# A written engine order through the first two feed-forward tiles of a two-layer cross-attention kernel

## The chip, the cores and the metric

The kernel runs on one core of a Trainium2 chip. The metric is the device time of one execution in microseconds (us); the time before is the median of three runs. One further execution was recorded by the hardware profiler, and the views quoted here come from it.

The core has a matrix engine (TensorE, "PE" in the profile, with its weight loads as "PEld"), a vector engine (VectorE, "DVE"), an activation engine (ScalarE, "ACT"), a third elementwise engine (GpSimd, "POOL") and a queue that issues transfers (SyncE, "SP").

## The reference

Two layers work on x, 8 batches of 112 tokens of 512 numbers, with a context of 375 rows for each batch. Each step normalises x first and adds its result to x.

```python
x = x + _L0_xattn_ref(_layernorm(x), ctx_2048, mask_BxS2_bk0)
x = x + _L0_ffn_ref(_layernorm(x), L0_ffn_w1, L0_ffn_w2, L0_ffn_w3)
x = x + _L1_xattn_ref(_layernorm(x), ctx_2048, mask_BxS2_ik0, L1_xattn_Wq, ...)
x = x + _L1_ffn_ref(_layernorm(x), L1_ffn_wq_gate, ...)
```

The change concerns the first two lines. Layer 0's attention has one head and no projections; masked scores are left out:

```python
scores = jnp.einsum('bsd,bmd->bsm', hidden_states, memory_tokens) * scale
attn = jax.nn.softmax(scores, axis=-1)
readout = jnp.einsum('bsm,bmd->bsd', attn, memory_tokens)
```

Layer 0's feed-forward rounds its activations to 8-bit steps for each token and its weights to -1, 0 and 1 times their mean magnitude (the straight-through terms change nothing in the value):

```python
def _act_quant(x):
    scale = 127.0 / jnp.clip(jnp.max(jnp.abs(x), axis=-1, keepdims=True), EPS)
    return jnp.clip(jnp.round(x * scale), -128, 127) / scale
def _weight_quant(w):
    scale = 1.0 / jnp.clip(jnp.mean(jnp.abs(w)), EPS)
    return jnp.clip(jnp.round(w * scale), -1, 1) / scale
def _bitlinear(x, w):
    xn = _rmsnorm(x)
    ...
    return jnp.einsum('bsd,hd->bsh', xq, wq)
gate = jax.nn.silu(_bitlinear(x, w1))
up = _bitlinear(x, w2)
return _bitlinear(gate * up, w3)
```

The hidden width is 1408. Layer 1's attention has 16 heads and needs, from the context, the keys and values of all 8 batches.

## The kernel before

The 896 tokens are handled by batch (8 of 112 rows) in layer 0's attention, and in 7 tiles of 128 rows from then on. `xs[i]` is tile i of the SBUF array `tokens`.

**Who decides the order.** Everything is written as a Python program for the engines. For PE and SP the written order is kept throughout. For DVE, ACT and POOL a planner orders the instructions by its own estimates, except inside a region opened with `tc.manual_schedule` that names these engines: there the written order is kept among the region's instructions, though planned ones from outside may be set between them. Before the change, such a region covers batches 1 to 7 of layer 0's attention and ends ahead of the feed-forward.

**Layer 0's attention.** For batch b, `write0` (DVE, L141) writes the normalised tokens h; `transpose0` turns them on PE (L358), with a copy on ACT (L360); `scores0` multiplies with the context (PE, L365 and L367), takes the row maximum (DVE, L371 and L372) and the exponential (ACT, L375); `shares0` inverts the sums (DVE, L380 and L381); `turn0` transposes the exponentials (PE, L387; ACT, L389); `readout0` multiplies with the context once more (PE, L394), adds to x (DVE, L396), and sends the result with a DMA from POOL's queue into `tokens` (L402). The tokens of x lie in three tiles of the pool `work0`: batch 0, batches 1 to 3, batches 4 to 7 (`load_x`).

**Filling PE.** The keys and values of layer 1 don't depend on layer 0. `fill(n)` takes the next n of their 56 steps: a key step is eight matmuls (L176) emptied by ACT (L178), a value step eight larger ones (L183), emptied in this stretch by DVE (L185). They are set between the steps of layer 0 to keep PE at work.

**The weights of layer 0.** `ternary(m)` is a generator for weight matrix m of three, stepped by `steps_of(m, n)`: four steps of Abs with a row sum (ACT, L230), one of totals (a small matmul L234 on PE, then DVE L236 to L240), four of scaling (DVE, L244) and Sign (ACT, L245). The list `BETWEEN` says for each batch b and each of three places n (after the scores, ahead of the fill, after `turn0`) which steps go there: a digit is a weight matrix, "p" a step of `preparing`.

**Preparing a feed-forward tile.** `prepare(i0, i1)` has four steps: batch statistics of the tiles' tokens and the inverse root (DVE, L128 to L119); the normalised tokens (DVE, L141), their squares (ACT, L263) and their largest magnitudes (DVE, L264); the rounding factors, a chain of small DVE operations (L267 to L278); the rounding itself (ACT, L305; DVE, L307). Before, `prepare(0, 2)` is stepped from `BETWEEN`, while `prepare(2, 4)` and `prepare(4, NT)` are written in the loop over tiles and are the planner's to place.

**The feed-forward tile.** `turn_gate0(i)` transposes the rounded tokens (PE, L317; ACT, L319). `gate_up0(i)` takes the hidden width in three blocks; each has a gate group and an up group of four matmuls (L501, two PSUM banks), Silu on ACT (L505) and the product on DVE (L506). It then finds the ranges (ACT L263, DVE L264 and a small chain), and rounds (ACT L512, POOL L515). `turn_down0(i)` transposes the result, and `down0(i)` multiplies with the third matrix (PE, L526) and adds to x (DVE, L528). The pool `ps_mm` has four PSUM banks, which gate, up, keys, values, read-outs and `down0` all share. The pool `work1` of these tiles takes the space that `work0` leaves.

Of the kernel before, what the change touches and what calls it, by code (L numbers as in the profile page):

```python
# [23 lines left out]
F32 = mybir.dt.float32  # L24
# [5 lines left out]
AF = mybir.ActivationFunctionType  # L30
# [32 lines left out]
def two_layers(ctx: ExitStack, tc: tile.TileContext, x, ctxT, ctxN, mask0, mask1, w1, w2, w3,  # L63
# [127 lines left out]
    def fill(n=1):  # L191
        for _ in range(n):
            next(kv_steps, None)
# [17 lines left out]
    with tc.tile_pool(name="w0", bufs=1, side="right") as w0p, \  # L211
# [68 lines left out]
            yield fwd, back  # L280

        rooms = {}

        def prepare(i0, i1):

            write = normaliser(xs[i0:i1], f"ln1{i0}")
            yield
            g = i0 // 4
            if g not in rooms:
                rooms[g] = slab("h1")  # L290
            js = range(i0 - 4 * g, i1 - 4 * g)
            hs = [rooms[g][:, j * D:(j + 1) * D] for j in js]
            qs = rooms[g][:, 4 * D:].bitcast(BF16)
            qs = [qs[:, j * D:(j + 1) * D] for j in js]
            for j in range(i1 - i0):
                write(hs[j], j)
            ranges = quantizers(hs, D, f"q1{i0}", qs)
            next(ranges)
            yield
            fwd, back = next(ranges)  # L300
            b1, b2 = back(means[0], 1), back(means[1], 2)
            yield
            for j in range(i1 - i0):
                backs[i0 + j] = b1[:, j:j + 1], b2[:, j:j + 1]
                nc.scalar.activation(hs[j], hs[j], AF.Identity, bias=rounder,  # L305
                                     scale=fwd[:, j:j + 1])
                nc.vector.tensor_scalar_sub(qs[j], hs[j], ROUND)  # L307
                q1[i0 + j] = qs[j]
            yield

        def transposed_h(q, n, name, pool):
            qT = pool.tile([P, n // P, P], BF16, name=f"{name}_qT", bufs=2)
            for c0 in range(0, n // P, 6):
                k = min(6, n // P - c0)
                pt = ps_s.tile([P, 6, P], BF16, name="s")
                for i in range(k):
                    nc.tensor.transpose(pt[:, i, :], q[:, (c0 + i) * P:(c0 + i + 1) * P],  # L317
                                        ident_h)
                nc.scalar.copy(qT[:, c0:c0 + k, :], pt[:, :k, :])  # L319
            return qT  # L320
# [5 lines left out]
        with tc.tile_pool(name="work0", bufs=2, side="right") as work0:  # L326
# [5 lines left out]
            cNs, normal, h0, hT0, s0, eT0 = {}, {}, {}, {}, {}, {}  # L332

            def load_x(b0, b1):
                t = work0.tile([T, b1 - b0, D], F32, name=f"x0_{b0}", bufs=1)
                nc.sync.dma_start(out=t, in_=x[b0:b1].rearrange("b t d -> t b d"))
                x0.extend(t[:, b, :] for b in range(b1 - b0))

# [95 lines left out]
            for i in range(4):  # L434
# [9 lines left out]

            BETWEEN = ["", "", "000", "0", "0", "1", "1", "0", "0", "0", "0", "1", "1", "1", "1",
                       "1", "1", "1p", "p", "2", "2p", "p", "2", "2"]
            preparing = prepare(0, 2)

            def between(b, n):
                for m in BETWEEN[3 * b + n]:
                    if m == "p":
                        next(preparing)
                    else:
                        steps_of(int(m), 1)

            with tc.manual_schedule(engines={ENGINES.PE, ENGINES.SP, ENGINES.DVE,
                                             ENGINES.Activation, ENGINES.Pool}):
                between(0, 2)  # L460
                for b in range(1, B):
                    if b < B - 1:
                        write0(b + 1)
                    scores0(b)
                    between(b, 0)
                    shares0(b)
                    if b > 1:
                        readout0(b - 1)
                    if b + 1 < B:
                        load_ctxN(b + 1)  # L470
                    if b + 2 < B:
                        cTs[b + 2] = load_ctxT(b + 2)
                    elif b + 2 == B:
                        cTs[2] = load_ctxT(2)
                    if b == 2 or b == 4:
                        load_raw(2, b // 2 - 1)
                    if b < B - 1:
                        transpose0(b + 1)
                    between(b, 1)
                    fill(1)  # L480
                    turn0(b)
                    between(b, 2)
                fill(1)
                turn_gate0(0)

                nc.scalar.activation(stat.tile([T, 1], F32, name="top"), s0[B - 1][1], AF.Silu)
                readout0(B - 1)


        with tc.tile_pool(name="work1", bufs=2, side="right") as work1:  # L490
            q3 = {}

            def gate_up0(i):
                qT = q1[i]
                gu = work1.tile([P, H], F32, name="gu")
                for n0, n in HBLK:
                    gate = ps_mm.tile([P, 512], F32, name="mm")
                    up = ps_mm.tile([P, 512], F32, name="mm")
                    for ps, w in ((gate, wqs[0]), (up, wqs[1])):
                        for kc in range(KC):  # L500
                            nc.tensor.matmul(ps[:, :n], lhsT=qT[:, kc, :],  # L501
                                             rhs=w[:, kc * H + n0:kc * H + n0 + n],
                                             start=(kc == 0), stop=(kc == KC - 1))
                    act = work1.tile([P, 512], F32, name="act")
                    nc.scalar.activation(act[:, :n], gate[:, :n], AF.Silu, scale=backs[i][0])  # L505
                    nc.vector.scalar_tensor_tensor(gu[:, n0:n0 + n], up[:, :n], backs[i][1],  # L506
                                                   act[:, :n], ALU.mult, ALU.mult)
                q = work1.tile([P, H], BF16, name="q3")
                ranges = quantizers([gu], H, "q3", [q])
                next(ranges)  # L510
                fwd, back = next(ranges)
                nc.scalar.activation(gu, gu, AF.Identity, bias=rounder, scale=fwd)  # L512
                for n0 in (0, H // 2):
                    cols = slice(n0, n0 + H // 2)
                    nc.gpsimd.tensor_scalar(q[:, cols], gu[:, cols], -ROUND, 1.0,  # L515
                                            ALU.add, ALU.mult)
                q3[i] = q, back

            def turn_down0(i):
                q3[i] = transposed_h(q3[i][0], H, "q3", work1), q3[i][1]  # L520

            def down0(i):
                qT, back = q3[i]
                o = ps_mm.tile([P, D], F32, name="mm")
                for hc in range(HC):
                    nc.tensor.matmul(o, lhsT=qT[:, hc, :], rhs=wqs[2][:, hc * D:(hc + 1) * D],  # L526
                                     start=(hc == 0), stop=(hc == HC - 1))
                nc.vector.scalar_tensor_tensor(xs[i], o, back(means[2], 3), xs[i], ALU.mult, ALU.add)  # L528

            for i in range(NT):  # L530
                if i == 2:
                    list(prepare(4, NT))
                gate_up0(i)
                if i == 0:
                    steps_of(2, 1)
                fill(1)
                if i == 0:
                    turn_gate0(1)
                    list(prepare(2, 4))
                fill(1)  # L540
                if i == 0:
                    steps_of(2, 1)
                elif i == 1:
                    steps_of(2, 2)
                if i:
                    turn_down0(i - 1)
                if 0 < i < NT - 1:
                    turn_gate0(i + 1)
                if i:
                    fill(1)  # L550

                if i == 1:
                    steps_of(2, 1)
                elif i == 2:
                    down0(0)
                if i > 1:
                    down0(i - 1)
                if i == 4:
                    wq_s = slab("wq")[:, :KC * D].rearrange("p (k d) -> p k d", k=KC)
                    nc.sync.dma_start(out=wq_s, in_=wq)  # L560
            write = normaliser(xs[:3], "ln2a")
            for i in range(3):
                transpose2(i, write, i, work1, ps_s)
            turn_down0(NT - 1)
            write = normaliser(xs[3:5], "ln2b")
            transpose2(3, write, 0, work1, ps_s)
            down0(NT - 1)
# [433 lines left out]
```

## Time and profile before

| | us |
|---|---|
| median of 3 runs | 538.13 (537.45 to 540.0) |
| the profiled execution | 537.93 |
| its span, from first to last instruction | 536.1 |
| PE busy | 516.8 |
| DVE busy | 312.1 |
| ACT busy | 247.2 |
| POOL busy | 91.4 |

The span is what the program's instructions cover; about 1.8 us lie around it. In the rows of the profile a name such as L176 is a line of the kernel; "x8" counts instructions; a bracket such as [1.54 <-DVE h L141] is idle time of the engine just ahead of the row and what ended it. A row of several matmuls is one that merges neighbours, so its length is a stretch and not the time of one.

### The profile page before, as it was taken

The numbers are of one execution on the slowest core, as the hardware profiler recorded it, in microseconds if no ns is written. First come the engines' busy times: TensorE is split into PE (matmuls) and PEld (weight loads), VectorE is DVE, ScalarE is ACT, GpSimd is POOL, SyncE is SP. The second block draws the span as 40 slices with busy tenths as digits, with TensorE's granted clock in tenths as the row PEclk, the third lists the DMA queues.
The fourth block names the chain that finished last, engine by engine and source line by source line (L and its number), as shares of the span: only waits on it lengthen the run. The fifth ranks groups of instructions, "written<-read, shape, count | busy, mean of one in ns | idle before, by whom it ended". The sixth has DMA issues, their size and how long they took to land.

```text
span 536.1 us, 8884 instructions
## 1 busy us (share of the span) xinstructions
PE 516.8 (96%) x3430; PEld 315.0 (59%) x3430; DVE 312.1 (58%) x769; ACT 247.2 (46%) x439; POOL 91.4 (17%) x197
## 2 busy tenths in 40 slices
PE   8998998989999999999999999999999999999995
PEld 6544554544455554545565555565654688889984
DVE  2552458769834755544546657988985764434432
ACT  1234754759644444402576545556766233203320
POOL 0000210101111101140121033523653540000000
PEclk9998999999999999999999999999999999999999
DMA  8994976300010120240123202102221000010001
GB/s 246 333 404 172 354 257 244 97 17 0 15 44 1 60 117 1 78 159 0 40 71 90 79 2 70 40 2 70 80 78 42 1 2 0 1 59 21 0 21 44
DMA packets 13312, 45.76 MB, mean 85 GB/s; under 512 B 1985, under 2 KB 2512, under 8 KB 12112
## 3 DMA queue, kind: packets, MB, share of 16 engines
q1 hardware_dynamic: 11744, 41.17, 22.5%
q0 software_dynamic: 1360, 3.96, 2.2%
q8 instruction: 29, 0.48, 0.4%
q14 instruction: 19, 0.16, 0.1%
q10 hardware_dynamic: 160, 0.01, 0.0%
HBM read 41.46 MB, written 1.84 MB: 81 GB/s over the span
## 4 chain that ended last, share of the span: by engine, by line
PE 82%; DVE 9%; issue 2%; ACT 2%; DMA 2%; POOL 2%; ACTq 0%; DVEq 0%; POOLq 0%
PE mm L183 14%; PE s L849 13%; PE mm L176 13%; PE down L867 7%; PE mm L648 5%; PE mm L600 5%; PE mm L501 4%; PE s L734 4%; PE mm L526 3%; PE s L365 3%; PE den L754 3%; PE mm L394 3%; PE num L759 2%; DMA tokens<-x 2%; DVE e L739 1%
## 5 line engine op out<-in xcount | busy, mean ns | idle before, releaser
L176 PE MATMUL mm<-cT,wk 128*128 128x375 f32 x256 | 88.8, 493 | 0.8 <-ACT act L505 0.8
L183 PE MATMUL mm<-wv,cT 128*125 128x512 f32 x192 | 86.8, 598 | 0.0
L740 ACT ACTIVATE e<-e 125x448 f32<-125x448 f32 x96 | 54.0, 574 | 45.3 <-DVE e L739 44.1
L849 PE MATMUL s<-h4T,w 128*128 128x512 f32 (+1 forms) x352 | 72.5, 367 | 1.2 <-DVE ln_f L95 1.2
L739 DVE TENSOR_SCALAR e<-s,upper 125x448 f32<-125x448 f32 x96 | 58.9, 677 | 18.8 <-PE s L734 18.8
L849 PEld LDWEIGHTS s<-h4T,w 128*128 128x128 f32 x352 | 63.5, 188 | 9.7 <-issue 1.8
L176 PEld LDWEIGHTS mm<-cT,wk 128*128 128x128 f32 x256 | 47.2, 192 | 29.2 <-issue 1.3
L183 PEld LDWEIGHTS mm<-wv,cT 128*125 128x125 f32 x192 | 34.8, 187 | 39.1 <-issue 37.5
L867 PE MATMUL down<-w,gu 128*128 128x512 f32 x154 | 37.0, 397 | 0.0
L501 PE MATMUL mm<-w_q,q_qT 128*128 128x512 fp8e4 (+1 forms) x168 | 34.6, 361 | 1.5 <-ACT act L505 1.5
L867 PEld LDWEIGHTS down<-w,gu 128*128 128x128 f32 x154 | 28.7, 188 | 6.6
L723 POOL TENSOR_SCALAR w<-raw 128x512 fp32r<-128x512 int32 (+1 forms) x35 | 22.3, 647 | 58.3 <-ACT w L721 57.9
L857 ACT CAST gu<-gu 128x512 fp32r<-128x512 f32 (+1 forms) x22 | 12.5, 568 | 40.5 <-DVE gu L855 40.5
L721 ACT ACTIVATE w<-raw,zero_point 128x512 fp32r<-128x512 int32 (+1 forms) x35 | 24.2, 694 | 10.6 <-DMA raw<-in_wd_dram 7.2
L734 PE MATMUL s<-qT,kv 32*125 32x112 f32 x768 | 28.5, 279 | 0.2
L501 PEld LDWEIGHTS <-q_qT 128*128 128x128 bf16 x168 | 16.4, 98 | 20.1 <-issue 2.8
L855 DVE SCALAR_TENSOR_TENSOR gu<-s,su,gu 128x512 f32<-128x512 f32 (+1 forms) x22 | 15.1, 684 | 22.2 <-PE s L849 20.2
L515 POOL TENSOR_SCALAR q<-gu 128x704 bf16<-128x704 f32 x14 | 10.9, 798 | 97.7 <-ACT gu L512 97.7
L734 PEld LDWEIGHTS s<-qT,kv 32*125 32x125 f32 x768 | 23.9, 183 | 6.2 <-issue 4.6
L759 PEld LDWEIGHTS num<-e,kv 125*32 125x32 f32 x768 | 20.5, 110 | 11.5 <-issue 11.0
L648 PE MATMUL mm<-wo,qT 128*128 128x512 f32 x56 | 25.8, 603 | 0.9 <-DVE qT L772 0.8
L402 POOL DMA_DIRECT2D tokens<-x x14 | 9.2, 657 | 100.0 <-DVE x L396 62.4
(210 smaller groups left out, 738.8 us busy)
## 6 DMA issues: line engine op xcount, KB each, us to landing
cT<-in_ctxT_dram SPq DMA_DIRECT2D x14, 750.0 KB, 5.6
raw<-in_w_dram SPq DMA_DIRECT2D x6, 1408.0 KB, 18.1
cN<-in_ctxN_dram SPq DMA_DIRECT2D x8, 768.0 KB, 4.7
raw<-in_wd_dram SPq DMA_DIRECT2D x11, 256.0 KB, 2.7
raw<-in_wg_dram SPq DMA_DIRECT2D x10, 256.0 KB, 2.9
raw<-in_wu_dram SPq DMA_DIRECT2D x10, 256.0 KB, 2.9
out_dram<-d SPq DMA_DIRECT2D x7, 256.0 KB, 2.0
wk<-in_wk_dram SPq DMA_DIRECT2D x2, 512.0 KB, 8.2
```

The costliest lines, as they stand in the source:

```text
L176: nc.tensor.matmul(ps, lhsT=wk_s[:, kc, dc * P:(dc + 1) * P], rhs=cT[:, kc, :], start=(kc == 0), stop=(kc == KC - 1))
L183: nc.tensor.matmul(ps, lhsT=cT[:, kc, c * CK:(c + 1) * CK], rhs=wv_s[:, kc, :], start=(kc == 0), stop=(kc == KC - 1))
L501: nc.tensor.matmul(ps[:, :n], lhsT=qT[:, kc, :], rhs=w[:, kc * H + n0:kc * H + n0 + n], start=(kc == 0), stop=(kc == KC - 1))
L600: nc.tensor.matmul(ps, lhsT=wq_s[:, kc, dc * P:(dc + 1) * P], rhs=h2T[g][:, kc, :], start=(kc == 0), stop=(kc == KC - 1))
L648: nc.tensor.matmul(ps, lhsT=qT[:, kc, i * P:(i + 1) * P], rhs=wo_s[:, kc, :], start=(kc == 0), stop=(kc == KC - 1))
L721: nc.scalar.activation(t, raw, AF.Square, bias=zero_point, accum_out=squares[:, k:k + 1])
L734: nc.tensor.matmul(ss[r][:, dc, :], lhsT=kT[rows, dc, c * CK:(c + 1) * CK], rhs=qT[rows, dc, b * T:(b + 1) * T], start=True, stop=True)
L739: nc.vector.tensor_scalar(e, ss[r], upper[:, c, b:b + 1], -CLIP, ALU.min, ALU.max)
L740: nc.scalar.activation(e, e, AF.Exp, scale=SC1)
L759: nc.tensor.matmul(num[r * HD:(r + 1) * HD, dc, :], lhsT=v[:, c, head], rhs=es[r][:, dc, :], start=(c == 0 and dc == 0), stop=(c == NCK - ...
L849: nc.tensor.matmul(ps[:, :n], lhsT=w[:, c:c + P], rhs=h4T[k][:, kc, :n], start=(kc == 0 and k == 0), stop=(kc == KC - 1 and k == 1))
L867: nc.tensor.matmul(ps, lhsT=gus[k][:, hc, j * P:(j + 1) * P], rhs=w[:, c:c + D], start=(hc == 0 and k == 0), stop=(hc == HC - 1 and k == 1))
```

## The change

The written region, which ended ahead of the feed-forward, is kept open in an `ExitStack` named `written` until after tile 1. Inside it, the three preparations are made ahead in a list `preparing`, and "P" in `BETWEEN` steps the second, as "p" steps the first. `gate_up0` is cut in three: `gate_up0` alone, `ranges0` and `round0`. Tiles 0 and 1 are written out, and the loop begins at tile 2. `write0` goes from one batch ahead to two. The tokens of batches 4 to 7 go from the pool `work0` into `w0p`, which lives until the end of layer 0's feed-forward. The order of the matmuls on PE is the same but for the totals of the first two weight matrices.

```diff
@@ prepare / load_x
         rooms = {}
+        written = ExitStack()
...
+        preparing = [prepare(0, 2), prepare(2, 4), prepare(4, NT)]
...
             def load_x(b0, b1):
-                t = work0.tile([T, b1 - b0, D], F32, name=f"x0_{b0}", bufs=1)
+
+                pool = w0p if b1 == B else work0
+                t = pool.tile([T, b1 - b0, D], F32, name=f"x0_{b0}", bufs=1)
@@ the batches
-            BETWEEN = ["", "", "000", "0", "0", "1", "1", "0", "0", "0", "0", "1", "1", "1", "1",
-                       "1", "1", "1p", "p", "2", "2p", "p", "2", "2"]
-            preparing = prepare(0, 2)
+            BETWEEN = ["", "", "000", "0", "1", "01", "1", "0", "0", "0", "0", "1", "1", "1", "1",
+                       "1", "1p", "", "p", "2", "2p", "p", "2P", "2"]
...
-            with tc.manual_schedule(engines={ENGINES.PE, ENGINES.SP, ENGINES.DVE,
-                                             ENGINES.Activation, ENGINES.Pool}):
-                between(0, 2)
-                for b in range(1, B):
-                    if b < B - 1:
-                        write0(b + 1)
-                    scores0(b)
...
+            written.enter_context(tc.manual_schedule(engines={
+                ENGINES.PE, ENGINES.SP, ENGINES.DVE, ENGINES.Activation, ENGINES.Pool}))
+            write0(2)
+            between(0, 2)
+            for b in range(1, B):
+                scores0(b)
+                between(b, 0)
+                shares0(b)
+                if b > 1:
+                    readout0(b - 1)
+                if b + 2 < B:
+                    write0(b + 2)
...
+            fill(1)
+            turn_gate0(0)
+
+            nc.scalar.activation(stat.tile([T, 1], F32, name="top"), s0[B - 1][1], AF.Silu)
+            next(preparing[1])
+            readout0(B - 1)
@@ gate_up0
+                q3[i] = gu
+
+            def ranges0(i):
+                gu = q3[i]
                 q = work1.tile([P, H], BF16, name="q3")
                 ranges = quantizers([gu], H, "q3", [q])
                 next(ranges)
-                fwd, back = next(ranges)
+                q3[i] = gu, q, *next(ranges)
+
+            def round0(i):
+                gu, q, fwd, back = q3[i]
                 nc.scalar.activation(gu, gu, AF.Identity, bias=rounder, scale=fwd)
@@ the tiles
-            for i in range(NT):
+            gate_up0(0)
+            next(preparing[1])
+            ranges0(0)
+            steps_of(2, 1)
+            fill(1)
+            turn_gate0(1)
+            next(preparing[1])
+            steps_of(2, 1)
+            round0(0)
+            fill(1)
+            steps_of(2, 1)
+            gate_up0(1)
+            ranges0(1)
+            steps_of(2, 1)
+            fill(1)
+            round0(1)
+            fill(1)
+            turn_down0(0)
+            turn_gate0(2)
+            steps_of(2, 1)
+            fill(1)
+            next(preparing[2])
+            written.close()
+            for i in range(2, NT):
                 if i == 2:
-                    list(prepare(4, NT))
+                    list(preparing[2])
                 gate_up0(i)
-                if i == 0:
-                    steps_of(2, 1)
-                fill(1)
...
+                ranges0(i)
+                round0(i)
+                fill(2)
+                turn_down0(i - 1)
+                if i < NT - 1:
+                    turn_gate0(i + 1)
                 fill(1)
...
```

More of the change, by code (lines that the diff above doesn't have):

```diff
@@ L443, in two_layers @@
             normal[2] = normaliser(x0[4:], "ln0c")
-            BETWEEN = ["", "", "000", "0", "0", "1", "1", "0", "0", "0", "0", "1", "1", "1", "1",
-                       "1", "1", "1p", "p", "2", "2p", "p", "2", "2"]
-            preparing = prepare(0, 2)
+            BETWEEN = ["", "", "000", "0", "1", "01", "1", "0", "0", "0", "0", "1", "1", "1", "1",
+                       "1", "1p", "", "p", "2", "2p", "p", "2P", "2"]
             def between(b, n):
                 for m in BETWEEN[3 * b + n]:
-                    if m == "p":
-                        next(preparing)
+                    if m in "pP":
+                        next(preparing["pP".index(m)])
@@ L455, in between @@
                     else:
                         steps_of(int(m), 1)
-            with tc.manual_schedule(engines={ENGINES.PE, ENGINES.SP, ENGINES.DVE,
-                                             ENGINES.Activation, ENGINES.Pool}):
-                between(0, 2)
-                for b in range(1, B):
-                    if b < B - 1:
-                        write0(b + 1)
-                    scores0(b)
[L465 to L479, printed above, removed]
-                    fill(1)
-                    turn0(b)
-                    between(b, 2)
-                fill(1)
-                turn_gate0(0)
-                nc.scalar.activation(stat.tile([T, 1], F32, name="top"), s0[B - 1][1], AF.Silu)
-                readout0(B - 1)
@@ new lines, in two_layers @@
+            written.enter_context(tc.manual_schedule(engines={
[10 more added lines that the diff above has]
+                    write0(b + 2)
+                if b + 1 < B:
+                    load_ctxN(b + 1)
+                if b + 2 < B:
+                    cTs[b + 2] = load_ctxT(b + 2)
+                elif b + 2 == B:
+                    cTs[2] = load_ctxT(2)
+                if b == 2 or b == 4:
+                    load_raw(2, b // 2 - 1)
+                if b < B - 1:
+                    transpose0(b + 1)
+                between(b, 1)
+                fill(1)
+                turn0(b)
+                between(b, 2)
@@ L528, in down0 @@
                 nc.vector.scalar_tensor_tensor(xs[i], o, back(means[2], 3), xs[i], ALU.mult, ALU.add)
-            for i in range(NT):
+            gate_up0(0)
[22 more added lines that the diff above has]
+            for i in range(2, NT):
                 if i == 2:
-                    list(prepare(4, NT))
+                    list(preparing[2])
                 gate_up0(i)
-                if i == 0:
-                    steps_of(2, 1)
-                fill(1)
[L537 to L554, printed above, removed]
+                ranges0(i)
[4 more added lines that the diff above has]
+                    turn_gate0(i + 1)
+                fill(1)
+                if i == 2:
                     down0(0)
-                if i > 1:
-                    down0(i - 1)
+                down0(i - 1)
                 if i == 4:
```

## The prediction

> **What bounds the kernel now.** I read the page first. Part 1 puts TensorE at 96% of a span of 536.1 us, and its second line of digits is 8 or 9 in every slice but the last: there is no stretch in which another engine carries the kernel. So an edit is worth what it takes from, or adds to, the time in which TensorE stands; and what TensorE loses once is not made up later.
>
> ```profile
> PE 516.8 (96%) x3430; PEld 315.0 (59%) x3430; DVE 312.1 (58%) x769; ACT 247.2 (46%) x439; POOL 91.4 (17%) x197
> ...
> PEclk9998999999999999999999999999999999999999
> ```
>
> The one 8 in the clock line is the slice from 40 to 54 us. Next, the waits of PE between 0 and 300 us (line waited for, total us, times, longest), without the start-up:
>
> ```profile
> PE s L234 <- ACT w_q L230: 2.3, 1, 2.3
> PE s L358 <- DVE h L141: 1.5, 1, 1.5
> PE mm L501 <- ACT act L505: 1.5, 1, 1.5
> ...
> PE mm L176 <- ACT act L505: 0.8, 1, 0.8
> ```
>
> All four lie in the stretch that the change rewrites. The timeline of PE shows the first, and that it costs more than its 2.35 us: the eight matmuls after it take 4.35 us where the same eight take 2.70 at 61.28.
>
> ```profile
> 38.68 0.60 PE L358 MATMUL s<-ident,h 112*128 112x112 f32 x4
> 41.63 0.39 PE L234 MATMUL s<-w_rows,ones 128*128 128x4 f32 x2 [2.35 <-ACT w_q L230]
> 41.87 4.35 PE L176 MATMUL mm<-cT,wk 128*128 128x375 f32 x8
> 46.02 0.63 PE L387 MATMUL s<-ident,e 112*125 112x112 f32 x3
> ```
>
> ScalarE's timeline has the third wait's cause (L505 waits for the tokens' DMA), and then the order in which it empties PSUM banks: L178 (keys) as soon as they are there, L505 in between, L512 (rounding) later.
>
> ```profile
> 113.59 1.27 ACT L505 ACTIVATE act<-mm,q_back 128x512 f32<-128x512 f32 x2 [3.72 <-DMA tokens<-x]
> ...
> 122.30 0.55 ACT L178 ACTIVATE kv<-mm,bk 128x375 f32<-128x375 f32 x1
> 122.76 0.67 ACT L505 ACTIVATE act<-mm,q_back 128x512 f32<-128x512 f32 x1
> ...
> 124.69 1.55 ACT L512 ACTIVATE gu<-gu,rounder,q_fwd 128x1408 f32<-128x1408 f32 x1
> ```
>
> [...] half speed from about 42.9 to 46.3, after the 2.35 us wait, and none after the waits of 1.5. [...]
>
> **What the change removes.** Each gain is a stretch between two PE starts, less the same stretch elsewhere.
> (A) The totals of the first weight matrix go behind a fill and behind turn0(1). Transposes to the next scores are 38.68 to 46.48 = 7.80; with a totals in it and no wait, 69.72 to 73.24 = 3.52. ScalarE ends the fourth Abs at 41.58, the fill covers that: gain 4.28. One Abs of the second matrix comes a step earlier; that matrix was not waited for at 47.05, and I charge nothing, with ScalarE's idle time before 46 as cover.
> (B) write0 goes an iteration ahead, and prepare(0,2) a step; prepare(2,4), which the planner had put into the same queue, goes to the last batch. The transpose then finds its h, written some 8 us before. 85.89 to 90.70 = 4.81 against 76.16 to 79.21 = 3.05: gain 1.76. The extra write0 per iteration (0.54 on DVE, ahead of nothing PE needs within 5 us) costs nothing. The DMA issues on SP (contexts, weights) and on POOL (tokens) keep their order and their places between the batches.
> (C) The tokens of batches 4 to 7 lie outside the space that act reuses. 109.18 to 115.62 = 6.44 against tile 3's 156.14 to 160.89 = 4.75: gain 1.69. The preparation in the last batches (two squares of 0.62, two maxima of 0.68, 13 small operations) lies beside read-out and fill, and ends about 1 us after gate_up0(0) begins, before its third block needs a bank.
> Sum 7.73: gate_up0(0) starts at about 103.14 and ends at 107.89.
>
> **What it adds.** Count from E, the end of tile 0's last product on DVE (L506), 0.89 after gate_up0 ends, as at tile 3. The written order now puts into DVE, one after another:
>
> ```profile
> 161.81 1.62 DVE L264 TENSOR_REDUCE q_mx<-gu 128x1 f32<-128x1408 f32 x1
> 163.37 0.15 DVE L267 TENSOR_SCALAR q_ss<-q_ss 128x1 f32<-128x1 f32 x1
> ...
> 165.87 0.16 DVE L274 SCALAR_TENSOR_TENSOR q_fwd<-q_fwd,q_y 128x1 f32<-128x1 f32 x1
> ```
>
> These rows are tile 3's, where nothing is interleaved: L506's end to the start of L512 takes 4.34. In tile 0, nineteen dependent small operations of prepare(2,4) stand ahead. Thirteen such start within 2.18 us at 28.45, so 0.18 each: 3.45. The factor of tile 0 is ready at E+7.8. Behind it: three operations of the totals 0.55, two L307 0.85, L244 0.94: E+10.15. ScalarE does Sign (L245, 1.40) only then, ahead of round0(0) (L512, 1.5): E+13.1. **Only behind that** stands the evacuation of the second key fill (L178, 0.55): E+13.65.
> PE comes sooner: totals, fill, transposes and fill took 115.62 to 121.18 = 5.56, and three groups of gate_up0(1) take 2.60, so it wants the fourth group's bank at E-0.89+8.16 = E+7.27. All four banks are then held: by the fill, and by three groups whose activations also queue behind it. Stall 6.4. Then another Sign (1.40) and L505 (0.67) free the fifth group at E+15.75, L506 (0.75) the sixth at E+16.5, and gate_up0(1) ends at E+17.15. Without a stall it would be E+9.42: 7.73 are lost here, by chance the sum gained. Before lost 0.94 here (121.18 to 126.87 against 4.75), so a lead of 0.94 is left.
> In tile 1 the chain is again in ScalarE's order. E1 = E+18.04; +4.34 factor, +0.94 L244, +1.40 Sign, +0.55 key, +1.5 round, +1.35 and +0.58 copies: the last, which gate_up0(2) reads, ends at E+28.75. PE needs 10.38 (126.87 to 137.25) and comes at E+27.53. Stall 1.2, so gate_up0(2) starts at 108.78+28.75 = 137.53 against 137.25: 0.28 late.
> Unknown costs, bounded. The clock: a 6.4 us stall takes it to half; the fifth and sixth groups (0.65 each) pay between 0 and 1.3. I take 0.65. Tile 2: prepare(4,7)'s first step (three L128, aggregates and the small chain, 4.35) is written ahead of gate_up0(2)'s first product. It starts at E+28.4 and ends at E+32.75; the sixth group then waits 0.75. If the planner puts three writes (0.5 each) and three maxima (0.6 each) ahead too, it waits 4.05. I take 2.4. A gain is excluded for both, since neither takes work away.
> Sum: 0.28 + 0.65 + 2.4 = 3.3 us longer, between 1.0 and 5.7. The profiled execution was 537.93 (span 536.1 and 1.8 around it), the median 538.13; the 0.2 between them is below everything here, so 538.13 + 3.3 = 541.5, with its own range 539.1 to 543.9.
>
> **Rivals.** *The gain stays* (529.5 to 535). If ScalarE reaches that key evacuation by E+7.3 instead of E+13.1, nothing stalls: 538.13-7.73-0.94 = 529.5. It decides at 6 us of queue time; half of it gives some 534. For it: every gain is a plain wait in the trace, while the loss is my walk through queues that do not exist yet, with operations in a row where the trace mostly shows them interleaved (0.07 apart). Against: L244 and both reductions are long rows, and three of four banks would still wait for L505.
> *One more wait* (543 to 546). Another of work0's tiles lies under act, so (C) stays, and DVE is backed up further in tile 2, where preparation of three tiles (about 8 us), tile 2's ranges (4.3) and two L528 (1.5) fall into some 14 us of PE.
> *The change doesn't do what it says* (537 to 540): if planned work still slips into the written stretch, as batch statistics did at 84 us, (B) and the stall both shrink.
>
> **Numbers.** About 0.5% (2.7 us) is what a measurement can tell from no change. Forecast 0.60: a third of it ends under 540.8 (same 0.19, slower 0.41). Gain stays 0.29, all faster. One more wait 0.07, slower. Does not do what it says 0.04, same. So faster 0.29, same 0.23, slower 0.48. The range, 531.5 to 545, leaves out the best part of the second case and the worst of the third.
>
> **What will show it.** (A): no 8 in the clock line at 40 us, L234 without a wait. (B): no wait of L358 for h. (C): no wait of L505 for tokens. The stall: PE waits 5 to 7 us in gate_up0(1) for L178 or L505, with L512 ahead of L178 on ScalarE, and an 8 or less in the clock slice at 120 us. Tile 2: waits of L501 for L319 and L506. I am wrong if L178 of the second fill comes before L512, or if PE waits under 2 us there.

## The result: no difference, though tile 0 ends eight microseconds earlier

| | before | after |
|---|---|---|
| median, us | 537.98 (20 runs) | 538.04 (20 runs, 537.08 to 538.71) |
| span of the profiled execution | 536.1 | 535.8 |
| ratio after / before | | 1.0003, 95% interval 0.9995 to 1.001 |

The forecast was 541.5. The executions of the kernel before are mostly of two kinds by granted clock: of the 39 that stood beside the first experiments below, 18 at 0.997 or 0.998 have a median of 537.2 us, and 18 at 0.994 or 0.995 one of 538.3.

The kernel after has line numbers of its own. In a feed-forward tile the matmuls L507, Silu L511, the product L512 and the rounding L525 are L501, L505, L506 and L512 of before; L306, L308, L320 and L322 are L305, L307, L317 and L319; the scores L370 are L365. The single parts below that start from the kernel before keep its numbers or are one off.

On the page of the kernel after, the line of the engines and that of the granted clock are these (columns: busy us, share of the span, instructions; then tenths in 40 slices of 13.4 us):

```profile
PE 516.7 (96%) x3430; PEld 314.3 (59%) x3430; DVE 316.0 (59%) x769; ACT 247.1 (46%) x439; POOL 93.4 (17%) x197
...
PEclk9999999997999999999999999999999999999999
```

The 8 at 40 us has gone, and a 7 has come at 121 us, a place where before had none. The waits of PE up to 300 us after (line waited for, us, times, longest) say the same:

```profile
PE mm L507 <- ACT kv L178: 5.5, 1, 5.5
```

The four waits of 2.3, 1.5, 1.5 and 0.8 us shown of before are all gone; one of 5.5 us is new. PE's timeline after (start, us, what ran), first at the old place of the totals, then at tiles 0, 1 and 2:

```profile
38.81 2.71 PE L176 MATMUL mm<-cT,wk 128*128 128x375 f32 x8
...
41.67 0.30 PE L234 MATMUL s<-w_rows,ones 128*128 128x4 f32 x2
...
102.78 4.92 PE L507 MATMUL mm<-w_q,q_qT 128*128 128x512 fp8e4 x24
107.53 0.28 PE L234 MATMUL s<-w_rows,ones 128*128 128x4 f32 x2
...
121.31 4.64 PE L507 MATMUL mm<-w_q,q_qT 128*128 128x512 fp8e4 x12 [5.47 <-ACT kv L178]
125.75 3.36 PE L176 MATMUL mm<-cT,wk 128*128 128x375 f32 x8
...
137.04 4.93 PE L507 MATMUL mm<-w_q,q_qT 128*128 128x512 fp8e4 x24 [0.17 <-ACT q_qT L322]
141.81 1.45 PE L183 MATMUL mm<-wv,cT 128*125 128x512 f32 x3
```

The same places before:

```profile
115.62 0.28 PE L234 MATMUL s<-w_rows,ones 128*128 128x4 f32 x2
...
126.87 2.79 PE L176 MATMUL mm<-cT,wk 128*128 128x375 f32 x8 [0.77 <-ACT act L505]
...
137.25 4.92 PE L501 MATMUL mm<-w_q,q_qT 128*128 128x512 fp8e4 x24
```

Take the start of the next row as the end of a group. `gate_up0(0)` ends at 107.53, where before it ended at 115.62: 8.09 us of lead. Tile 1 ends at 125.75 (126.87 before: 1.12 left), tile 2 starts at 137.04 (137.25: 0.21 left) and ends at 141.81 (142.01: 0.20 left). From there on both kernels do the same, and the spans differ by 0.3. So eight microseconds were won ahead of tile 0 and given back within tiles 0 and 1. ScalarE's timeline after shows where:

```profile
117.88 1.47 ACT L245 ACTIVATE w_q<-raw,unrounder 128x1408 fp8e4<-128x1408 f32 x1 [4.87 <-DVE raw L244]
119.25 1.54 ACT L525 ACTIVATE gu<-gu,rounder,q_fwd 128x1408 f32<-128x1408 f32 x1
120.70 0.56 ACT L178 ACTIVATE kv<-mm,bk 128x375 f32<-128x375 f32 x1
```

ScalarE stands for 4.87 us with a Sign at the head of its queue that waits for VectorE. The key fill, finished on PE at 113.09, has its bank emptied (L178) only behind that Sign and behind the rounding (L525). PE's next group needs this bank. ScalarE is idle in these 4.87 us, while the finished bank waits from 113.09 to 120.70; it is held by the row at the head of its written order. That row's input is late on VectorE, whose timeline has the scaling that Sign reads only behind the chains of small operations for tiles 2 and 3 and for tile 0, whose factor is the first row here:

```profile
115.70 0.16 DVE L274 SCALAR_TENSOR_TENSOR q_fwd<-q_fwd,q_y 128x1 f32<-128x1 f32 x1
...
116.90 1.81 DVE L244 TENSOR_SCALAR raw<-raw,w_scale 128x1408 f32<-128x1408 f32 x2
```

### The profile page after: what moved, and what is told of

Its sections match the earlier page's. It is cut to its first block, busy times and chain, and to the rows that moved or that the text cites. A ratio compares the mean times of both kernels' runs of the same rounds, so it can differ in the third digit from the quotient of the medians.

```text
span 535.8 us, 8871 instructions
## 1 busy us (share of the span) xinstructions
PE 516.7 (96%) x3430; PEld 314.3 (59%) x3430; DVE 316.0 (59%) x769; ACT 247.1 (46%) x439; POOL 93.4 (17%) x197
## 4 chain that ended last, share of the span: by engine, by line
PE 86%; DVE 8%; ACT 3%; POOL 1%; issue 1%; DVEq 0%; POOLq 0%
PE mm L183 14%; PE s L871 13%; PE mm L176 12%; PE down L889 7%; PE mm L507 6%; PE mm L670 5%; PE mm L622 5%; PE mm L399 4%; PE s L370 4%; PE s L756 4%; PE mm L539 3%; PE den L776 3%; PE num L781 2%; DVE e L761 1%; PE s L428 1%
## 5 line engine op out<-in xcount | busy, mean ns | idle before, releaser
L176 PE MATMUL mm<-cT,wk 128*128 128x375 f32 x256 | 87.7, 488 | 0.0
L176 PEld LDWEIGHTS mm<-cT,wk 128*128 128x128 f32 x256 | 47.1, 191 | 28.1 <-issue 1.2
L507 PE MATMUL mm<-w_q,q_qT 128*128 128x512 fp8e4 (+1 forms) x168 | 36.8, 376 | 5.7 <-ACT kv L178 5.5
L507 PEld LDWEIGHTS <-q_qT 128*128 128x128 bf16 x168 | 16.8, 101 | 26.0 <-issue 9.0
L407 POOL DMA_DIRECT2D tokens<-x x14 | 11.8, 843 | 90.9 <-DVE x L401 62.9
```

The source lines that it names most:

```text
L176: nc.tensor.matmul(ps, lhsT=wk_s[:, kc, dc * P:(dc + 1) * P], rhs=cT[:, kc, :], start=(kc == 0), stop=(kc == KC - 1))
L507: nc.tensor.matmul(ps[:, :n], lhsT=qT[:, kc, :], rhs=w[:, kc * H + n0:kc * H + n0 + n], start=(kc == 0), stop=(kc == KC - 1))
```

## The experiments

Two theories stood against each other. **Order**: the gains ahead of tile 0 are real and add up, and the written order of tiles 0 and 1 gives them back. **Work**: VectorE and ScalarE have too much to do beside PE in these tiles, so any earlier start ends in a wait there, whatever the order. Each run below stood beside runs of the kernel before on the same chip (538.05 or 538.13); ratios are to those.

### The gains one at a time

**a_totals**: the kernel before, with the totals of the first weight matrix behind the fill and `turn0(1)`; the nine steps of the second matrix each come one place earlier, and the preparation stays where it was.

```diff
-BETWEEN = ["", "", "000", "0", "0", "1", "1", ... "1", "1", "1p", "p", ...
+BETWEEN = ["", "", "000", "0", "1", "01", "1", ... "1", "1", "p", "p", ...
```

> The kernel before with only the totals of the first weight matrix moved behind the fill and turn0 of batch 1 (one Abs of the second matrix a step earlier, one step of prepare a place later); the rest stays the planner's. Theory (each wait taken away is worth its own length, and the change gave the sum back in tiles 0 and 1): PE no longer waits 2.35 us for L230 and the clock stays full, so 4.3 us shorter, about 533.7. Rival (something later sets the time, so an earlier gain is lost anyway): within 1 us of 538.

Measured 534.67, ratio 0.9947 (0.9926 to 0.9968). PE's timeline:

```profile
38.75 0.60 PE L358 MATMUL s<-ident,h 112*128 112x112 f32 x4
39.19 2.71 PE L176 MATMUL mm<-cT,wk 128*128 128x375 f32 x8
...
42.05 0.30 PE L234 MATMUL s<-w_rows,ones 128*128 128x4 f32 x2
42.20 2.76 PE L365 MATMUL s<-cT,hT 128*112 128x375 f32 x8
```

No bracket, and the eight L176 take 2.71 (4.35 before, with a granted clock of 0.50 from 44 to 46 us). Transposes to the next scores: 3.45 us instead of 7.80. Of these 4.35 us, 3.4 reach the median. The next run shows one reason for the rest: the half clock behind the 2.35 us wait, worth 1.6 of them, is missing in that trace.

**c_tokens_pool**: the kernel before, with only the tokens of batches 4 to 7 in `w0p`.

```diff
-t = work0.tile([T, b1 - b0, D], F32, name=f"x0_{b0}", bufs=1)
+pool = w0p if b1 == B else work0
+t = pool.tile([T, b1 - b0, D], F32, name=f"x0_{b0}", bufs=1)
```

> The kernel before with only the tokens of batches 4 to 7 in the pool w0p. Theory: the wait of L505 for the tokens' DMA goes and with it 1.7 us of PE in gate_up0(0), about 536.3; the planner's order behind it may take some of that. Rival: another tile of work0 lies under act, the wait stays, 538.

Measured 536.43, ratio 0.9969 (0.9957 to 0.9981). The gain is 1.6. PE's timeline, at the totals and at tile 0 (L502 is L501 of before):

```profile
42.26 0.38 PE L234 MATMUL s<-w_rows,ones 128*128 128x4 f32 x2 [2.35 <-ACT w_q L230]
42.50 2.77 PE L176 MATMUL mm<-cT,wk 128*128 128x375 f32 x8
...
108.39 4.92 PE L502 MATMUL mm<-w_q,q_qT 128*128 128x512 fp8e4 x24
113.15 0.28 PE L234 MATMUL s<-w_rows,ones 128*128 128x4 f32 x2
```

PE no longer waits for the first activation of tile 0: 108.39 to 113.15 is 4.76, against 6.44 before. The first two rows are not the edit's doing: the wait for the totals is as long as before (2.35), but the eight matmuls behind it take 2.77 and not 4.35, at a granted clock of 1.00. So this gain is read from the medians and from tile 0, not from the two spans.

**b_write_ahead**: the kernel before, with only `write0` two batches ahead and one "p" a place earlier.

```diff
-BETWEEN = [... "1", "1", "1p", "p", ...
+BETWEEN = [... "1", "1p", "1", "p", ...
+write0(2)
 between(0, 2)
 for b in range(1, B):
-    if b < B - 1:
-        write0(b + 1)
     scores0(b)
...
         readout0(b - 1)
+    if b + 2 < B:
+        write0(b + 2)
```

> Only (B): write0 two batches ahead and the second step of the first preparation one place earlier; the totals, the tokens' pool and the tiles as before. Theory (the three gains are separate waits and add up): the wait of L358 for h goes, 1.76 us by my sum, 536.4; what the two other single parts leave of close_early's 6.1 us (6.1 - 3.4 - 1.6) says 1.1, 537.0. Rival (the h is late for another reason, the preparation that the planner still sets into VectorE's queue): the wait of 1.5 us stays, 538.1.

Measured 539.44, ratio 1.0023 (1.0012 to 1.0034): **slower**, and neither theory had it. PE's timeline has the wait for h gone, and two others in its place:

```profile
93.48 0.58 PE L387 MATMUL s<-ident,e 112*125 112x112 f32 x3 [0.96 <-ACT e L375]
95.12 2.78 PE L365 MATMUL s<-cT,hT 128*112 128x375 f32 x8 [1.06 <-ACT hT L360]
```

VectorE's timeline of the same run says why (before, these two rows start at 86.78 and 90.12):

```profile
86.88 0.69 DVE L128 BATCH_NORM_STATS2 bn<-tokens 128x6 f32<-128x512 f32 x1 [3.73 <-DMA tokens<-x]
...
91.23 0.54 DVE L371 TENSOR_REDUCE top<-s 112x1 f32<-112x375 f32 x1
```

`prepare(2, 4)` is the planner's in this kernel, and it was set into the queue so early that VectorE stands 3.73 us for the tokens' transfer (0.28 at this row before). A value copy (L185) and a scaling (L244), which before ran ahead of the statistics, now come behind their chain of small operations and ahead of the row maximum L371 of scores that were finished at 86. So (B) is worth its 1.76 only together with the set place for that preparation; the change has both, and the stretch that was 4.81 before takes 3.05 in the kernel after (81.25 to 84.30).

### Keeping the gains, with the tiles left to the planner

**close_early**: the kernel after, with the written region closed behind `readout0(B - 1)`; tiles 0 and 1 have the same PE order as after, and the planner orders the other engines.

```diff
         next(preparing[1])
         readout0(B - 1)
+        written.close()
...
             next(preparing[2])
-            written.close()
```

> The changed kernel with the written region ended ahead of gate_up0(0), so that the planner orders tiles 0 and 1 as it did before; the earlier totals, the earlier write0, the earlier preparation and the tokens' pool stay. The planner's order of ScalarE has one Sign ahead of the second key evacuation, where the written one had two roundings, Sign and round0(0), but it has the squares and roundings of tiles 4 to 6 ahead of the activations of gate_up0(2). Theory: the lead of 8 us shrinks by 1 to 3 us in tile 1 and 3 to 5 in tile 2, 532 to 536. Rival (a planned order has no cost here): 529.5.

Measured 532.01, ratio 0.9883 (0.9868 to 0.9898): the lower end of what was expected. PE's waits inside the tiles are small:

```profile
PE mm L507 <- ACT act L511: 1.4, 2, 0.8
...
PE mm L507 <- DVE kv L185: 0.5, 1, 0.5
```

The planner's order of ScalarE has the second key fill emptied at 115.53, where the written one had it at 120.70:

```profile
115.53 0.56 ACT L178 ACTIVATE kv<-mm,bk 128x375 f32<-128x375 f32 x1
```

The same instructions on the same engines, but for the order of DVE, ACT and POOL in two tiles: 6.0 us between this and the kernel after. This is against **Work**.

### Which place in the order

**key_first**: after, with the second key fill directly behind `turn_gate0(1)`, so that L178 stands ahead of Sign and rounding.

```diff
 turn_gate0(1)
+fill(1)
 next(preparing[1])
 steps_of(2, 1)
 round0(0)
-fill(1)
```

> The changed kernel with the second key fill of tile 0 written ahead of the rounding of tiles 2 and 3, of Sign and of round0(0): PE's order is the same, ScalarE empties that bank at once. Theory (all of ScalarE's queue is late, not one bank): the stall of 5.5 us only moves from the fourth group of gate_up0(1), where it ended with L178, to the fifth, where it ends with L511; one group of 0.87 us gets done ahead of it, so 0.4 to 0.9 us shorter, 537.1 to 537.6. Rival (that one evacuation is the bound): most of 5.5 us comes back, 532.5 to 534.

Measured 538.04, ratio 1.0001 (0.999 to 1.0012). In the waits of PE the stall is as long, one bank later:

```profile
PE mm L507 <- ACT act L511: 6.1, 1, 6.1
```

L511 of tile 1 is now what stands behind Sign, rounding and Sign. That the stall would move was expected; the half microsecond of gain was not found.

**gate_first**: after, with the fill and all of `gate_up0(1)` ahead of both Signs and `round0(0)`.

```diff
 turn_gate0(1)
+fill(1)
 next(preparing[1])
+gate_up0(1)
 steps_of(2, 1)
 round0(0)
-fill(1)
 steps_of(2, 1)
-gate_up0(1)
```

> The changed kernel with the second key fill and gate_up0(1) written ahead of both Sign steps and of round0(0), nothing else moved; PE's order is the same. Theory (ScalarE's order, not PE's, sets these tiles): gate_up0(1) stalls less than 1 us, and ends some 7 us earlier, but the rounding and Sign steps put off now end before tile 2's copy all the same, so PE stalls 5 to 6 us ahead of gate_up0(2), and 1 to 2 us of the whole are left: 536 to 537. Rival (the stall in gate_up0(1) was the whole loss): 530 to 532.

Measured 537.6, ratio 0.9992 (0.9985 to 0.9999). PE's timeline:

```profile
134.50 4.91 PE L507 MATMUL mm<-w_q,q_qT 128*128 128x512 fp8e4 x16 [5.67 <-DVE ln_b L107]
```

Tile 1 runs without a wait, and the stall has gone to the next tile, as expected; of the 1 to 2 us that were to be left of the whole, the medians have 0.4. The releaser that the bracket names is not the one: what `gate_up0(2)` reads is the last copy of ScalarE, and ScalarE's timeline has it behind a Sign that waited for VectorE:

```profile
129.30 1.47 ACT L245 ACTIVATE w_q<-raw,unrounder 128x1408 fp8e4<-128x1408 f32 x1 [3.64 <-DVE raw L244]
...
132.58 1.86 ACT L322 COPY q_qT<-s 128x768 bf16<-128x768 bf16 x3
```

The copies end at 134.44, and PE starts at 134.50. It is the chain that the forecast gave for tile 1, here with nothing ahead of it to hide it.

**hold_tile2**: after, with `gate_up0(2)` inside the written region, behind the first step of `prepare(4, NT)`. This puts to the test the forecast's last term, in which that step stands ahead of tile 2's products.

```diff
+            gate_up0(2)
             written.close()
             for i in range(2, NT):
                 if i == 2:
                     list(preparing[2])
-                gate_up0(i)
+                else:
+                    gate_up0(i)
```

> The changed kernel with the written region ended behind gate_up0(2) instead of ahead of it: the three products of that tile can no longer slip between the batch statistics of tiles 4 to 6. Theory (that slip is why the 2.4 us forecast for tile 2 did not come): a wait of 0.8 to 2 us in gate_up0(2), 538.8 to 540. Rival (the statistics have room there in any order): 538.0.

Measured 539.09, ratio 1.0016 (1.0008 to 1.0025). The waits of PE:

```profile
PE mm L183 <- DVE gu L512: 1.2, 1, 1.2
```

VectorE's timeline has the three products only behind the whole step:

```profile
142.79 2.08 DVE L512 SCALAR_TENSOR_TENSOR gu<-mm,q_back,act 128x512 f32<-128x512 f32 x3
```

This is the wait that the forecast had put into the kernel after, one group later (at the value fill behind the tile); it comes on top of the 5.5 us for L178, and the median is 1.05 us above that of the kernel after.

### An order that keeps the gains

**reordered**: the ranges of tile 0 ahead of the preparation, both key fills ahead of the rounding, totals and scalings of the third matrix behind `gate_up0(1)`; what follows tile 1's steps is planned.

```diff
             gate_up0(0)
-            next(preparing[1])
             ranges0(0)
             steps_of(2, 1)
             fill(1)
             turn_gate0(1)
+            fill(1)
             next(preparing[1])
-            steps_of(2, 1)
             round0(0)
-            fill(1)
-            steps_of(2, 1)
             gate_up0(1)
-            ranges0(1)
-            steps_of(2, 1)
+            next(preparing[1])
             fill(1)
-            round0(1)
+            steps_of(2, 2)
+            ranges0(1)
             fill(1)
             turn_down0(0)
             turn_gate0(2)
+            round0(1)
             steps_of(2, 1)
             fill(1)
-            next(preparing[2])
             written.close()
             ...
                 gate_up0(i)
+                if i == 2:
+                    steps_of(2, 1)
```

> The changed kernel with the same steps in tiles 0 and 1 in another written order: ranges of tile 0 first, both key fills ahead of round0(0), the factors of tiles 2 and 3 next to it, gate_up0(1) ahead of the rounding of tiles 2 and 3 and of all Sign steps, round0(1) behind the transposes; preparation of tiles 4 to 6 left to the planner. PE's order is the same. Theory: no bank waits in gate_up0(1) nor in gate_up0(2), and the lead of some 8 us at the start of tile 0 and 0.9 more of tile 1 is kept: 529 to 531. Rival (the lead is lost in any order, because ScalarE and VectorE have too much to do in these tiles): 536 to 539.

Measured 536.95, ratio 0.998 (0.9967 to 0.9993): 6 us above the 529 to 531 that were expected. VectorE's timeline:

```profile
108.13 0.69 DVE L128 BATCH_NORM_STATS2 bn<-tokens 128x6 f32<-128x512 f32 x1 [2.30 <-DMA tokens<-x]
...
118.20 1.50 DVE L244 TENSOR_SCALAR raw<-raw,w_scale 128x1408 f32<-128x1408 f32 x1
```

This L128 is a statistic of tiles 4 to 6, where the kernel after begins them at 137.52. It was outside the region, so the planner set it, with its normalisation and maxima, between the written rows; VectorE stood 2.30 us for a transfer, the scaling (the second row) came late, and tile 1's products came only at 122.32. PE stood 3.2 us for them, and 2.2 us for activations:

```profile
123.12 4.48 PE L176 MATMUL mm<-cT,wk 128*128 128x375 f32 x8 [3.17 <-DVE gu L512]
```

**written_to_tile2**: the same list, with tile 2, the last Sign and the first step of `prepare(4, NT)` inside the region too, in that order. Against reordered:

```diff
             fill(1)
+            gate_up0(2)
+            steps_of(2, 1)
+            next(preparing[2])
             written.close()
             for i in range(2, NT):
                 if i == 2:
                     list(preparing[2])
-                gate_up0(i)
-                if i == 2:
-                    steps_of(2, 1)
+                else:
+                    gate_up0(i)
```

> The other written order once more (ranges of tile 0 first, both key fills ahead of round0(0), gate_up0(1) ahead of the rounding of tiles 2 and 3 and of all Sign steps, round0(1) behind the transposes), but the written region reaches past gate_up0(2), with the last Sign step and the first step of prepare(4,7) behind it, so that the planner can set nothing of tiles 4 to 6 ahead of the products of tiles 0 and 1. Theory (the reordered kernel kept only 1 us because planned work of tiles 4 to 6 stood ahead of written products on VectorE): no wait of gate_up0(1), 1 to 2 us in gate_up0(2), 530 to 532. Rival (these two engines have no room for the work in any order): 535 to 538.

Measured **531.24**, ratio 0.9863 (0.9848 to 0.9879). PE's timeline:

```profile
118.97 2.79 PE L176 MATMUL mm<-cT,wk 128*128 128x375 f32 x8 [0.32 <-DVE gu L512]
...
129.36 5.03 PE L507 MATMUL mm<-w_q,q_qT 128*128 128x512 fp8e4 x24
...
154.25 4.06 PE L176 MATMUL mm<-cT,wk 128*128 128x375 f32 x12 [0.98 <-ACT act L511]
```

Tile 2 starts at 129.36, where both kernels have 137. PE runs the same rows in the same order here as in the kernel after; only the orders of VectorE, ScalarE and GpSimd differ, and the pages count the same instructions (769 and 439). **Order** it is. ScalarE's timeline gives the cause of the last wait:

```profile
151.40 2.22 ACT L306 ACTIVATE h<-h,rounder,q_fwd 128x512 f32<-128x512 f32 x3 [1.29 <-DVE q_fwd L274]
153.53 1.13 ACT L511 ACTIVATE act<-mm,q_back 128x512 f32<-128x512 f32 x2
```

**rounding_later**: those three roundings written behind `gate_up0(3)`. Against written_to_tile2:

```diff
                 if i == 2:
-                    list(preparing[2])
+                    next(preparing[2])
+                    next(preparing[2])
                 else:
                     gate_up0(i)
+                if i == 3:
+                    list(preparing[2])
```

> written_to_tile2 with the roundings of tiles 4 to 6 written behind tile 3's gate_up0 instead of ahead of it. Theory: what was left there, 0.98 us of PE for L511 behind the three L306, goes: 530.3, ratio to before 0.9845. Rival: the planner sets the three L306 by its own estimates and leaves them where they were, or they now make the transposes of tile 4 late (L320 for L308): 531.2 or more.

Measured **530.05**, ratio 0.9843 (0.9827 to 0.986). The wait is gone from PE's timeline:

```profile
153.10 5.22 PE L176 MATMUL mm<-cT,wk 128*128 128x375 f32 x16
```

This is the best version found: 1.6% under the kernel before.

## Why the prediction was wrong, point by point

**The gains (A), (B), (C)** were right. Forecast start of `gate_up0(0)` 103.14, measured 102.78; lead at its end 7.73 against 8.09. In the kernel after the three stretches take 3.45, 3.05 and 4.75 us, where the forecast had 3.52, 3.05 and 4.75; of the 0.36 us that are over, PE had 0.31 already at 38.37, ahead of all three. The single runs give -3.4 for (A) and -1.6 for (C). (A) was priced from an execution with half clock behind its wait (4.35 us for the eight L176), which a wait of the same 2.35 us did not bring in c_tokens_pool (2.77). (B) hangs on the set place of `prepare(2, 4)`: I had charged nothing for leaving the planner's queue, which is right for the change and would have been wrong for (B) by itself.

**The stall** was right in place, cause and order: PE waits for L178 of the second key fill, which stands behind L525. The forecast had taken ScalarE to start no row ahead of an earlier one that waits; in this trace that holds (L178 behind 4.87 us of an idle ScalarE), and b_write_ahead has the same for VectorE (L371 at 91.23, on scores finished at 86, behind a wait of 3.73). Its size was 5.47 against 6.4. From E (108.42 here), PE came for the bank at E+7.42 (forecast E+7.27); the evacuation ended at E+12.84 (forecast E+13.65). The factor was ready at E+7.44 (E+7.8), the first Sign began at E+9.46 (E+10.15).

**Tile 1's chain on ScalarE** was right in its order, and in its end by some luck: its last copy was to free `gate_up0(2)` at E+28.75, and that started at E+28.62. Against the forecast, the evacuation came 0.81 us sooner, the stretch from there to tile 1's last product was 1.03 longer (5.42 for 4.39), and the chain behind it 0.35 shorter (10.36 for 10.71).

**The clock** was mis-sized. The windows of the kernel after (columns: PE, PEld, DVE and ACT and POOL busy us with their counts, granted clock, DMA share, GB/s):

```profile
116.00:121.00 5.00, 0.00 (x0) 0.00 (x0) 2.79 (x7) 3.12 (x3) 0.11 (x1) 0.93 0.00 0
121.00:123.00 2.00, 1.69 (x4) 0.55 (x4) 0.00 (x0) 2.00 (x3) 1.42 (x2) 0.50 0.00 0
```

It stays at 0.50 to 127 and is 0.97 from 127 to 129; with 0.70 us from the first window and 0.12 from the last, half speed lasts 6.8 us, not the two groups that I counted. From 121.31, the second half of tile 1 takes 4.44, where the forecast had 3.5, and the fill behind it 3.20 where the one at 107.67 takes 2.61: 0.94 and 0.59 us, against my 0.65. The two do not count alike. ScalarE's chain starts from tile 1's last product, so the 0.94 delayed the chain with PE; it is most of the 1.03 above. The 0.59 lies behind that start. In the forecast PE was to stand 1.2 us for the chain ahead of `gate_up0(2)`; PE came later and stood 0.17, so these 0.59 cost the end nothing.

**Tile 2** is the step that failed: "prepare(4,7)'s first step [...] is written ahead of gate_up0(2)'s first product", and "I take 2.4". VectorE's timeline after:

```profile
138.33 0.67 DVE L128 BATCH_NORM_STATS2 bn<-tokens 128x6 f32<-128x512 f32 x1
139.09 0.75 DVE L512 SCALAR_TENSOR_TENSOR gu<-mm,q_back,act 128x512 f32<-128x512 f32 x1
...
139.85 0.66 DVE L128 BATCH_NORM_STATS2 bn<-tokens 128x6 f32<-128x512 f32 x1
```

The products of tile 2 are outside the region, so the planner set them between the written rows: the first behind the second of three statistics, the second at 140.85 ahead of the small chain. My text had the rule ("planned ones from outside may be set between them") and used it only against the change: for planned writes and maxima that come ahead, not for the products. My range for this term, 0.75 to 4.05, had no zero in it, because both its ends put the products behind the statistics; that the edit "takes no work away" excludes a gain and says nothing on that. hold_tile2 shows the step from the other side: with the products held behind the statistics, the wait of 1.2 appears and the kernel is 1.05 us slower. So even where the step holds, 2.4 was twice too much.

The sum, then: forecast 0.28 + 0.65 + 2.4 = +3.3. With its first two terms the forecast had `gate_up0(2)` 0.93 us later than before; it starts 0.21 earlier. These 1.1 us are the start of tile 0 (0.36 sooner), the evacuation (0.81 sooner) and the chain (0.35 shorter), less 0.38 by which the stretch with the half clock exceeded my 0.65. The third term is 0 where I had 2.4, and the spans differ by 0.3. So of the 3.5 us by which the forecast was off, 2.4 lie in tile 2 and 1.1 ahead of it. That the loss in tiles 0 and 1 comes out so near to the 8.09 won is luck as far as the runs show; the forecast said the same of its own two numbers.

**The rivals.** "The gain stays" was decided by whether ScalarE reaches the evacuation in time; in the kernel after it does not, and in close_early, written_to_tile2 and rounding_later the gain did stay, 6 to 8 us of it. "The change doesn't do what it says" has the right time (537 to 540) with another mechanism: the stretch that was written was kept, and the interleaving that saved the time lies just behind it.

## What to carry to other kernels

When an engine's order is written out, walk its rows up to the one that frees a PSUM bank, and look at what its predecessors wait for: in the kernel after a Sign that waits 4.87 us for VectorE holds back the emptyings written behind it (L178 until 120.70, L511 until 122.52), and moving rows ahead of it only handed the stall to the next bank (6.07 us in key_first) or the next tile (5.67 us in gate_first). A written region needs both its ends checked, since planned work from outside falls between its rows, with its own waits for transfers (2.30 us in reordered, 3.73 us in b_write_ahead) or to advantage (the kernel after). And where a loss on one engine stands ahead of its wait for another, ask where the other's chain starts: a loss ahead of that start delays both (the 0.94 us in tile 1), one behind it is used up by the wait (the 0.59 us on the fill).

## What the hardware showed that was not expected

Half clock lasted 3.4 us in three traces and twice that in two. From windows of 0.5 to 5 us, each share under 1.00 taken as time at 0.50: before 3.4 us (with a wait of 2.35), reordered 3.4 (3.17), gate_first 3.4 (5.67), the kernel after 6.8 (5.47), key_first 6.8 (6.07). The longer wait did not always go with the longer half speed: beside 5.67 us in gate_first it was 3.4, and beside 5.47 in the kernel after 6.8. Behind the two waits of 1.5 us before there was none (1.00 from 85 to 95 and from 110 to 125 us). In the kernel after the half speed begins some 1.0 us before the end of the wait (0.50 in 120.3 to 121), so part of it is spent on nothing.

A wait of 2.35 us for the totals was followed by half clock in one trace and not in another. Before, behind the wait, which ends at 41.63 (columns as above):

```profile
42.00:44.00 2.00, 2.00 (x6) 1.19 (x6) 0.92 (x4) 0.00 (x0) 0.00 (x0) 0.73 0.99 408
44.00:46.00 2.00, 2.00 (x4) 1.00 (x3) 0.00 (x0) 0.00 (x0) 0.00 (x0) 0.50 0.73 301
46.00:48.00 2.00, 2.00 (x9) 1.35 (x8) 0.00 (x0) 1.74 (x3) 0.00 (x0) 0.92 0.08 33
```

In c_tokens_pool, where the wait ends at 42.26:

```profile
37.55:40.96 3.41, 2.36 (x10) 1.04 (x8) 0.78 (x3) 1.89 (x5) 0.00 (x0) 1.00 1.03 368
40.96:44.37 3.41, 2.12 (x8) 1.47 (x9) 1.16 (x6) 1.66 (x3) 0.00 (x0) 1.00 0.97 407
```

In b_write_ahead the same wait of 2.35 us was again followed by slow matmuls: the eight L176 behind it take 4.24 us, where the eight at 61.25 take 2.70. What decides whether such a wait brings half clock, and for how long, is not shown: only one execution of each kernel has a trace.
